# A two-layer max-aggregating graph network and an expert block: two tiles' late maxima and convolutions moved beside the last block steps of each layer

## The chip, the cores and the metric

The kernel runs on one core of one Trainium2 chip. A core has five engines that each work through their own instructions in order: TensorE (PE, matrix products), VectorE (DVE, elementwise work and maxima), ScalarE (ACT, copies and activations), GpSimd (POOL, here almost only the issuer of indirect gathers) and SyncE (SP, the issuer of plain transfers). PEld is TensorE's weight load. The metric is device time in microseconds (us); lower is better.

## The reference

1250 nodes with 512 features each, 20,000 random edges. The graph part is two layers of the same form, on layer-normalised rows:

```python
def _graph_conv_max(x, src, dst, W_rel, b, W_root):
    agg = jax.ops.segment_max(x[src], dst, num_segments=N)
    agg = jnp.where(jnp.isfinite(agg), agg, 0.0)
    return agg @ W_rel.T + b + x @ W_root.T
h = jax.nn.relu(_graph_conv_max(x, src, dst, W1_rel, b1, W1_root))
h = jax.nn.relu(_graph_conv_max(h, src, dst, W2_rel, b2, W2_root))
```

For every node this is the elementwise maximum over the rows of its neighbours, times one weight matrix, plus the node's own row times another. The result is added to `x`. Then comes an expert block: router logits, a softmax over the nodes, the top 512 nodes of each of eight experts, two matrix products per expert and a scatter back.

## The kernel before, in words

The nodes stand in NT = 10 tiles of TN = 125. Each layer has two phases, and the order of the instructions on each engine is the order of the program: a wrapper pins each call in program order (its line 34 is why every row of the profile says L34; rows are told apart by their buffers).

**The maximum of a tile** has three sources. *Block steps*: for destination tile t and source tile b, TensorE multiplies one-hot matrices (`ohs`) with the rows held as three bf16 parts (`xh`), six products into a PSUM bank of 125x1024; VectorE takes the maximum into `acc`. There are 10 x 10 steps, counted by `done`; step 10t+b+1 is the pair (t, b), its first step (b = 0) is copied by ScalarE, its last is followed by a fold (L640). Three PSUM banks (`pq` twice, `pair`) let TensorE run ahead. *Own rows*: what the blocks don't hold, seven gathered rows per node, from `table_d` by the index `nat_i`, as one group of four and one of three. *Late rows*: for nodes with still more neighbours; ten lists of falling length (34 down to 2), 30 groups of at most four rows; the maximum of each list goes to the DRAM tensor `late_d` (`ovf_d` in the profile), and every tile later gathers one row of it by `slot_i`.

**The first phase** (`first_phase`, L665) walks through a list of groups while the block steps run. Group n of `groups` is gathered by POOL into one of four `hb` buffers as soon as one is free, and merged by VectorE once `done` has reached `due`:

```python
due = lead + BEFORE + (n_steps - lead - BEFORE) * n // len(groups)
```

In layer one (lead 12) there are 34 groups: 30 late ones, n = 0 to 29, and the own groups of tiles 3 and 4, n = 30 to 33. Their due steps from n = 29 on are 87, 90, 92, 95, 97. In layer two (lead 10) there are 40: the same 30, then the own groups of tiles 0 to 4; due from n = 29 on are 76, 78, 80, 82, 84, 87, 89, 91, 93, 95, 97. The last late list, n = 29, has a single group of two rows; VectorE merges it and SyncE stores it to `late_d`. Before the last group is gathered, POOL asks for the late rows of tiles 0 to 3, four gathers into `wroot`, which has held W_root until then. Between the steps, pieces of the root product (`root_part`: the own row times W_root, stored to `root_d`) are handed out so that all are out at step 85.

**The second phase** (`second_phase`, L787) finishes the tiles. `own_rest(t)` gathers and merges the seven own rows of tiles 5 to 9, `backs` takes the late row into `acc`, and `ended(t)` transposes `acc` (`turn`), multiplies by W_rel (`conv`: eight products of 512 columns, four chunks by two passes, and the addition of the stored root part by an identity product) and hands over to a generator: in layer one `hidden` (ReLU, store to the other table, three bf16 parts), in layer two `residual` (ReLU plus `x`, moments, normalised row to `y_d`, transposed, logits). `on()` moves each waiting generator by one stage. The gathers of the second phase are 5 x 7 own rows and 6 late rows, 41 in all, on POOL's queue in program order, into the same four `hb` buffers. PSUM banks for transposes and for products are one each while the blocks run (`deep`), two each afterwards.

Of the kernel before, what the change touches and what calls it, by code (L numbers as in the profile page):

```python
# [23 lines left out]
class InOrder:  # L24


    def __init__(self, tc, engine):
        self.tc, self.engine = tc, engine
# [13 lines left out]
def fast_gnn(tc, ctx, sh, io, y_d):  # L42
# [283 lines left out]
    def turned(rows, dest):  # L326
        pt = bank("t")
        for c in range(KC):
            pe.transpose(pt[:, c, :TN], rows[:, c * P:(c + 1) * P], ident[:TN, :TN])
        act.copy(dest, pt[:, :, :TN])  # L330
# [202 lines left out]
    def grouped(rows):  # L533
        return [rows[j:j + G] for j in range(0, len(rows), G)]

    def own(layer, t):
        return [(table_d[layer], nat_i[:, t, k:k + 1]) for k in range(K0)]
# [102 lines left out]
    def block_steps(with_own):  # L640

        for t in range(NT):
            for b in range(NB):
                pq = bank("q")
                for r in range(R):
                    oh = ohs[:BR, t, (b * R + r) * TN:(b * R + r + 1) * TN]
                    for k in range(3):
                        pe.matmul(pq[:TN, r, :], oh, xh[:BR, b, k, :], start=(k == 0), stop=(k == 2))
                yield
                if b == 0:  # L650
                    acc2 = gk.tile([P, R, D], F32, name="acc2", bufs=2)
                    act.copy(acc2[:TN], pq[:TN])
                else:
                    dve.tensor_max(acc2[:TN], acc2[:TN], pq[:TN])
                if b == NB - 1:
                    if t in with_own:
                        folded(acc2, acc2[:TN, 0, :])
                        dve.tensor_max(acc[:TN, t, :], acc[:TN, t, :], acc2[:TN, 0, :])
                    else:
                        folded(acc2, acc[:TN, t, :])  # L660
                yield

    BEFORE = 4

    def first_phase(layer, lead, groups, lists, blocks, done):  # L665

        here = range(0 if layer else FRONT, NT)
        roots = in_turn([root_part(layer, t) for t in here])  # L670
        n_steps, given = NT * NB, 0
        def step():
            nonlocal done, given
            if layer == 0 and done % NB == 4 and done // NB + 2 < NT:
                onehots(done // NB + 2)
            if layer == 0 and done == NB + 2:
                own_early(2)
            next(blocks)
            done += 1
            while given < done * ROOT_PIECES * len(here) * 100 // (85 * n_steps):  # L680
                next(roots, None)
                given += 1
            next(blocks)

        deep[0] = True
        while done < lead:
            step()
        for n, (rows, i, fresh, whole) in enumerate(groups):
            due = lead + BEFORE + (n_steps - lead - BEFORE) * n // len(groups)
            for k in range(NT):  # L690
                if len(lists) < min(n + 3, NT) and k not in lists:
                    late_list(k)
                    lists.add(k)
            if 2 * n > len(groups) and weights[layer][2] is None:
                load_rel(layer)
            if n + 1 == len(groups):

                for k in range(G):
                    pool.indirect_dma_start(
                        out=wroot[:, k, :], out_offset=None, in_=late_d[:, :],  # L700
                        in_offset=bass.IndirectOffsetOnAxis(ap=slot_i[:, k:k + 1], axis=0))
            hb_g = gathers(rows)
            while done < due:
                step()
            if fresh:
                aw = wide()
            if len(rows) < 4 and fresh:
                dve.tensor_max(aw[:TN, 0, :], hb_g[0][:TN, 0, :], hb_g[0][:TN, 1, :])
                assert len(rows) == 2
                whole(aw, False)  # L710
                continue
            merged(hb_g, aw, fresh)
            if whole:
                whole(aw, True)
        while done < n_steps:
            step()
        deep[0] = False
        for _ in roots:
            pass
# [5 lines left out]
    def own_groups(layer, tiles):  # L725
        groups = []
        for t in tiles:
            parts_ = grouped(own(layer, t))
            for k, rows in enumerate(parts_):
                whole = (lambda aw, both, t=t: joined(aw, t)) if k + 1 == len(parts_) else None  # L730
                groups.append((rows, None, k == 0, whole))
        return groups

    def late_groups(layer):
        groups = []

        def kept(aw, both, i):
            ao = aw[:, 0, :]
            if both:
                ao = gk.tile([P, D], F32, name="line", bufs=LINES)  # L740
                folded(aw, ao[:TN])
            stored(late_d[i * TN:(i + 1) * TN, :], ao)

        for i in range(NT):
            parts_ = [[(layer, i, k) for k in range(CAPS[i])][j:j + G] for j in range(0, CAPS[i], G)]
            for k, rows in enumerate(parts_):
                whole = (lambda aw, both, i=i: kept(aw, both, i)) if k + 1 == len(parts_) else None
                groups.append((rows, i, k == 0, whole))
        return groups

    def conv(layer, t, agT):
        pm = bank("m")
        for c in range(KC):
            pe.matmul(pm[:TN], agT[:, c, :], weights[layer][2][:, c, :], start=(c == 0), stop=False)
        pe.matmul(pm[:TN], ident[:TN, :TN], ahead.pop(t)[:TN], start=False, stop=True)
        return pm
# [27 lines left out]
        head.logits(t, bank("t").rearrange("p c n -> p (c n)"))  # L784
        yield

    def second_phase(layer, finish, beside, between):  # L787

        going, turns = [], {}

        def on():
            for g in list(going):
                if next(g, True):
                    going.remove(g)

        def own_rest(t):
            aw = wide()
            for k, rows in enumerate(grouped(own(layer, t))):  # L800
                merged(gathers(rows), aw, k == 0)
            joined(aw, t)

        def backs(tiles, hb=None):
            if hb is None:
                hb, _ = gathers([(late_d, slot_i[:, t:t + 1]) for t in tiles])
            for k, t in enumerate(tiles):
                dve.tensor_max(acc[:TN, t, :], acc[:TN, t, :], hb[:TN, k, :])

        def turn(t):  # L810
            turns[t] = gk.tile([P, KC, TN], F32, name="turn", bufs=3)
            turned(acc[:TN, t, :], turns[t])

        def ended(*tiles):
            for t in tiles:
                if t not in turns:
                    turn(t)
                if t + 1 in ready:
                    turn(t + 1)
                g = finish(t, conv(layer, t, turns.pop(t)))  # L820
                next(g)
                on()
                if t + 1 == NT:
                    next(g)
                going.append(g)

        backs((0, 1, 2, 3), wroot)
        ready = {0, 1, 2, 3}
        ended(0)
        own_rest(5)  # L830
        ended(1)
        backs((4, 5))
        ready |= {4, 5}
        ended(2)
        own_rest(6)
        ended(3)
        own_rest(7)
        backs((6, 7))
        ready |= {6, 7}
        ended(4)  # L840
        own_rest(8)
        ended(5)
        own_rest(9)
        ended(6)
        backs((8, 9))
        ready |= {8, 9}
        beside()
        for t in (7, 8, 9):
            ended(t)
            between(t)  # L850
        while going:
            on()
            between(NT)

    first_phase(0, 12, late_groups(0) + own_groups(0, range(KEPT, EARLY)), set(),
                block_steps(set(range(KEPT))), 0)
    pbad = bank("m")
    pe.matmul(pbad[:1, :1], bads, ones_col, start=True, stop=True)
    dve.tensor_scalar(flag_i, pbad[:1, :1], 1.0, None, op0=ALU.min)
# [12 lines left out]
        for t in range(5):  # L872
            ready_block(t)

    second_phase(0, hidden, begun, ready_block)
    first_phase(1, 10, late_groups(1) + own_groups(1, range(EARLY)), set(range(NT)), blocks, ready_steps[0])

    words = ohs.rearrange("p t n -> p (t n)").bitcast(F32)[:, KC * N:]
    x_tiles = [words[:, k * D:(k + 1) * D] for k in range(6)]
# [11 lines left out]
        if t < NT:  # L891
            sp.dma_start(x_tiles[t % 6][:TN], x[t * TN:(t + 1) * TN, :])

    for t in range(3):
        fetch_x(t)
    head.load()

    def dense_begun():
        head.load_dense()
        head.constants()  # L900

    second_phase(1, residual, dense_begun, lambda t: head.begin(1) if t == NT else None)
    head.softmax()
    gctx.close()
    return acc, yT, flag_i, head
# [350 lines left out]
class Routing:  # L1256
# [180 lines left out]
    def beside(self, n=1):  # L1437
        for _ in range(n):
            next(self.steps, None)
# [404 lines left out]
```

## Time and profile before

| | |
|---|---|
| time, median of 3 runs | 889.24 us (889.02 to 891.01) |
| profiled execution's own time | 889.6 us |
| its span, first to last instruction | 887.9 us |
| mean granted TensorE clock | 0.942 |
| busy: PE / DVE / POOL / ACT | 695.0 / 629.2 / 533.5 / 159.5 us |
| gathers by the late lists / by own rows, on POOL | 214 at 1073 ns / 140 at 1057 ns |
| layer one: first phase ends (last fold), layer two's blocks alone begin | 303.2, about 390 us |
| layer two: first phase ends, last tile's convolution is under way | 600.6, about 675 us |

A row of the timeline has the start in us, the duration in us, the engine, the line, the operation, what it writes and reads, the shape, the count, and in brackets the idle time of the engine just before it with what ended that idle time. "issue" in the bracket means that nothing the profile shows was waited for. A group of rows with the same form that follow each other is merged. Gathers by POOL show the time of the issue; the data lands later. A product that writes `pq` or `pair` from `xh,ohs` is a block step; `acc<-acc,pq` is its maximum.

### The profile page before, as it was taken

How to read it: one execution, taken by the hardware profiler on the slowest of the kernel's cores; microseconds unless marked ns; L12 is line 12 of the kernel's file. 1: busy time of each engine (PE TensorE's matmuls, PEld its weight loads, DVE VectorE, ACT ScalarE, POOL GpSimd, SP SyncE). 2: the span in 40 equal slices, each digit the busy share in tenths (PEclk: the TensorE clock that was granted, in tenths of full speed). 3: DMA queues.
4: the chain of work that ended last, by engine and by line, in shares of the span. 5: the costliest groups of instructions: out<-in, count | busy, mean ns of one | idle time of the engine just before them, and what ended most of it. 6: DMA issues, size and time to landing. Idle time of an engine off the chain costs nothing. (4 is left out here: it accounts for less than half of the span.)

```text
span 887.9 us, 8334 instructions
## 1 busy us (share of the span) xinstructions
PE 695.0 (78%) x2534; PEld 374.1 (42%) x2534; DVE 629.2 (71%) x1156; ACT 159.5 (18%) x285; POOL 533.5 (60%) x547
## 2 busy tenths in 40 slices
PE   0599856777878688789788789758877888999992
PEld 0344433444445333345444445434434444444441
DVE  7799899999999945639899799987743554233211
ACT  2633000001000033130001011001223322112110
POOL 7552777777776876037777777777721401566542
PEclk9999989999999699899999999988989997999997
DMA  7676467978777588237977878877851404777753
GB/s 164 203 242 209 120 197 173 228 224 244 230 219 207 165 255 271 70 109 203 170 251 219 266 245 268 246 231 214 258 184 49 143 0 163 169 181 175 132 103 51
DMA packets 67784, 165.46 MB, mean 186 GB/s; under 512 B 12918, under 2 KB 17588, under 8 KB 67730
## 3 DMA queue, kind: packets, MB, share of 16 engines
q0 software_dynamic: 37472, 114.19, 49.1%
q1 hardware_dynamic: 29438, 49.55, 17.4%
q10 hardware_dynamic: 820, 1.10, 0.5%
q8 instruction: 22, 0.36, 0.2%
q14 instruction: 32, 0.26, 0.1%
HBM read 136.35 MB, written 28.40 MB: 186 GB/s over the span
## 5 line engine op out<-in xcount | busy, mean ns | idle before, releaser
L34 POOL DMA_INDIRECT hb<-table_d,late_i x214 | 229.6, 1073 | 105.4 <-issue 55.3
L34 PEld LDWEIGHTS <-ohs 126*125 126x125 bf16 (+1 forms) x1221 | 168.5, 139 | 226.1 <-issue 149.2
L34 PE MATMUL pq<-xh,ohs 126*125 126x512 bf16 x816 | 204.3, 393 | 57.8 <-DVE acc L34 47.4
L34 POOL DMA_INDIRECT hb<-table_d,nat_i x140 | 147.9, 1057 | 57.5 <-issue 36.9
L34 DVE TENSOR_TENSOR acc<-acc,pq 125x1024 f32<-125x1024 f32 x122 | 148.5, 1218 | 26.3 <-PE pq L34 19.5
L34 PE MATMUL pair<-xh,ohs 126*125 126x512 bf16 x384 | 96.1, 387 | 30.9 <-DVE acc L34 30.9
L34 POOL DMA_INDIRECT ysel<-y_d,idx x28 | 27.7, 988 | 77.4 <-issue 31.5
L34 DVE TENSOR_TENSOR acc<-acc,pair 125x1024 f32<-125x1024 f32 x58 | 70.5, 1216 | 3.8 <-PE pair L34 1.6
L34 DVE TENSOR_TENSOR wide<-wide,hb 125x1024 f32<-125x1024 f32 (+1 forms) x60 | 71.4, 1190 | 2.4 <-DMA hb<-table_d,late_i 0.6
L34 DVE TENSOR_TENSOR hb<-hb 125x1024 f32<-125x1024 f32 (+2 forms) x55 | 52.8, 961 | 24.9 <-DMA hb<-table_d,nat_i 18.0
L34 PE MATMUL pm<-wroot,turn 128*125 128x512 f32 x128 | 66.8, 607 | 0.4 <-ACT turn L34 0.4
L34 PE MATMUL pm<-yselT,w 128*128 128x512 f32 x112 | 52.4, 623 | 4.7 <-ACT yselT L34 4.7
L34 POOL DMA_INDIRECT out<-oo,idx x28 | 44.8, 1600 | 15.8 <-DVE oo L34 8.1
L34 PE MATMUL pm<-w,hT 128*128 128x512 f32 x112 | 52.7, 591 | 0.0
L34 DVE TENSOR_SCALAR oo<-pm,val 128x512 f32<-128x512 f32 x28 | 21.0, 751 | 44.0 <-PE pm L34 44.0
L34 DVE TENSOR_TENSOR wide<-hb 125x1024 f32<-125x1024 f32 (+1 forms) x40 | 47.8, 1196 | 4.9 <-DMA hb<-table_d,nat_i 3.4
L34 PE MATMUL pair<-wrel,turn 128*125 128x512 f32 x80 | 41.5, 667 | 9.9 <-ACT turn L34 7.7
L34 PE MATMUL pm<-wrel,turn 128*125 128x512 f32 x80 | 40.5, 653 | 3.3 <-DVE acc L34 3.3
L34 DVE COPY got<-pi 128x20 f32<-128x20 f32 x7 | 1.2, 178 | 52.4 <-PE pi L34 52.4
L34 PEld LDWEIGHTS pm<-yselT,w 128*128 128x128 f32 x112 | 21.6, 199 | 31.5 <-issue 25.0
L34 ACT COPY line<-pm 125x512 f32<-125x512 f32 x16 | 9.4, 586 | 137.4 <-PE pm L34 121.1
L34 PE MATMUL pair<-ident,acc 125*128 125x125 f32 x48 | 8.7, 312 | 32.2 <-ACT acc L34 18.5
(268 smaller groups left out, 877.5 us busy)
## 6 DMA issues: line engine op xcount, KB each, us to landing
w<-in_fw SPq DMA_DIRECT2D x14, 512.0 KB
ohs<-idx_d SPq DMA_DIRECT2D x10, 615.2 KB
root_d<-line SPq DMA_DIRECT2D x20, 250.0 KB
ahead<-root_d SPq DMA_DIRECT2D x20, 250.0 KB
table_d<-acc SPq DMA_DIRECT2D x20, 224.0 KB
ovf_d<-line SPq DMA_DIRECT2D x18, 224.0 KB
hb<-table_d,late_i POOLq DMA_INDIRECT x214, 5.1
ohs<-in_x SPq DMA_DIRECT2D x10, 250.0 KB
```

What stands on the lines that cost most here:

```text
L34: made = call(*args, **kwargs)
```

## The change

`second_phase` becomes a class `SecondPhase` that exists before the first phase starts, and `first_phase` takes `hooks`: functions called after given block steps.

- Layer one: after step 95 the late maxima of tiles 0 and 1, after step 96 `ended(0)`, after 98 the late maxima of tiles 2 and 3, after 99 `ended(1)`.
- Layer two: after step 75 the loads of three tiles of `x` and of the router weights, after 88 the late maxima of tiles 0 and 1, after 90 `ended(0)`, after 95 `ended(1)`, after 96 the late maxima of tiles 2 and 3. The root pieces are handed out by step 72 there.
- The four gathers of late rows into `wroot` stand before the gathers of group n = 31 (`n_late + 1`) in both layers, and any root pieces left are handed out ahead of them. Before, that was n = 33 in layer one and n = 39 in layer two.
- The rest of the second phase begins with two gathers, the late rows of tiles 4 and 5, into `wroot`, and goes on with tile 2.

```diff
-    def first_phase(layer, lead, groups, lists, blocks, done):
+    def first_phase(layer, lead, groups, n_late, lists, blocks, done, rooted, hooks):
...
-            while given < done * ROOT_PIECES * len(here) * 100 // (85 * n_steps):
+            while given < done * ROOT_PIECES * len(here) * 100 // (rooted * n_steps):
                 next(roots, None)
                 given += 1
             next(blocks)
+            if done in hooks:
+                hooks[done]()
...
-            if n + 1 == len(groups):
+            if n == n_late + 1:
+                for _ in roots:
+                    given += 1
 
                 for k in range(G):
                     pool.indirect_dma_start(
...
-        backs((0, 1, 2, 3), wroot)
-        ready = {0, 1, 2, 3}
-        ended(0)
-        own_rest(5)
-        ended(1)
-        backs((4, 5))
-        ready |= {4, 5}
-        ended(2)
-        own_rest(6)
-        ended(3)
...
+        def rest(self, beside, between):
+            late = wroot[:, 0:2]
+            for k in range(2):
+                pool.indirect_dma_start(
+                    out=late[:, k, :], out_offset=None, in_=late_d[:, :],
+                    in_offset=bass.IndirectOffsetOnAxis(ap=slot_i[:, 4 + k:5 + k], axis=0))
+            self.ended(2)
+            self.own_rest(5)
+            self.backs((4, 5), late)
+            self.ended(3)
+            self.own_rest(6)
+            self.ended(4)
+            self.own_rest(7)
+            self.backs((6, 7))
+            self.ended(5)
+            self.own_rest(8)
+            self.ended(6)
+            self.own_rest(9)
+            self.backs((8, 9))
+            beside()
+            for t in (7, 8, 9):
+                self.ended(t)
+                between(t)
...
+    second = SecondPhase(0, hidden)
+    first_phase(0, 12, late_groups(0) + own_groups(0, range(KEPT, EARLY)), len(late_groups(0)), set(),
+                block_steps(set(range(KEPT))), 0, 85,
+                {95: lambda: second.backs((0, 1), wroot), 96: lambda: second.ended(0),
+                 98: lambda: second.backs((2, 3), wroot[:, 2:4]), 99: lambda: second.ended(1)})
...
+    first_phase(1, 10, late_groups(1) + own_groups(1, range(EARLY)), len(late_groups(1)), set(range(NT)),
+                blocks, ready_steps[0], 72,
+                {75: head_begun, 88: lambda: layer2.backs((0, 1), wroot), 90: lambda: layer2.ended(0),
+                 95: lambda: layer2.ended(1), 96: lambda: layer2.backs((2, 3), wroot[:, 2:4])})
```

The order of `ended`, `on`, `backs`, `turn` and `own_rest` inside is the same as before, except that `ended` takes one tile and `backs` notes the tiles that are ready.

## The prediction

> **What bounds the kernel now.** I read the windows by stage first, then POOL's timeline where the moved gathers stand, then VectorE's beside it, then TensorE's convolution, and the same for layer two. The windows show microseconds, then busy time and count per engine:
>
> ```profile
> 278.00:303.20 25.20, 15.97 (x65) 9.12 (x63) 24.12 (x26) 1.01 (x1) 17.60 (x17) 0.87 0.69 195
> 303.20:354.50 51.30, 43.85 (x114) 20.58 (x115) 29.50 (x40) 15.29 (x27) 38.69 (x34) 0.87 0.79 239
> ...
> 545.90:600.60 54.70, 37.63 (x150) 21.72 (x147) 49.94 (x51) 3.44 (x5) 42.52 (x41) 0.90 0.80 242
> 600.60:655.00 54.40, 42.61 (x144) 22.67 (x145) 40.14 (x73) 13.02 (x30) 38.84 (x52) 0.91 0.75 229
> ```
>
> The columns after the length are PE, PEld, DVE, ACT, POOL. At the end of a first phase VectorE is full (24.12 of 25.20 us). In a second phase no engine looks full, but POOL's 38.7 us leave out 0.30 us of issue at each of 34 gathers: it has no real gap. So **first phases go at VectorE's pace and second phases at POOL's**. Now POOL in layer one:
>
> ```profile
> 269.55 0.95 POOL L34 DMA_INDIRECT hb<-table_d,nat_i  x1 [0.30 <-issue]
> 270.80 0.95 POOL L34 DMA_INDIRECT hb<-table_d,nat_i  x1 [0.30 <-issue]
> ...
> 278.86 0.95 POOL L34 DMA_INDIRECT hb<-table_d,nat_i  x1 [0.30 <-DMA ovf_d<-line]
> 282.83 1.36 POOL L34 DMA_INDIRECT wroot<-ovf_d,slot_i  x1 [3.03 <-DMA ovf_d<-wide]
> ...
> 287.49 1.15 POOL L34 DMA_INDIRECT wroot<-ovf_d,slot_i  x1 [0.30 <-issue]
> 288.94 0.95 POOL L34 DMA_INDIRECT hb<-table_d,nat_i  x1 [0.30 <-DVE acc L34]
> ...
> 291.45 0.94 POOL L34 DMA_INDIRECT hb<-table_d,nat_i  x1 [0.30 <-DMA wroot<-ovf_d,slot_i]
> ```
>
> 265.80 to 269.55 are the four rows of group 30, 270.80 to 273.30 the three of 31, 275.07 to 278.86 the four of 32. Then the late rows wait 3.03 us until the store of the last late list (`ovf_d<-wide`) has landed at 282.8. The reader is to see that POOL runs ahead of VectorE, and what is late when it gets there:
>
> ```profile
> 277.05 0.69 DVE L34 TENSOR_TENSOR wide<-hb 125x512 f32<-125x512 f32 x1
> ...
> 284.42 0.69 DVE L34 TENSOR_TENSOR hb<-hb 125x512 f32<-125x512 f32 x1
> ```
>
> 277.05 is the merge of group 29, at its due step 87; its store is issued at 277.76. 284.42 is the merge of group 31. Layer two, with the same marks:
>
> ```profile
> 540.32 0.94 POOL L34 DMA_INDIRECT hb<-table_d,nat_i  x1 [0.30 <-issue]
> 545.24 0.69 DVE L34 TENSOR_TENSOR wide<-hb 125x512 f32<-125x512 f32 x1
> 545.96 0.74 SPq L34 DMA_DIRECT2D ovf_d<-wide  x2
> ...
> 552.70 0.68 DVE L34 TENSOR_TENSOR hb<-hb 125x512 f32<-125x512 f32 x1
> ```
>
> POOL stands at group 31 (540.32) 5.6 us before the store it will now have to wait for is even issued.
>
> **The moved gathers, layer one.** All times below are on the clock of the profiled execution. Nothing before step 87 changes, so the store still lands at 282.8. In the new order POOL reaches the late rows after group 30, at 270.5, and stands for **12.3 us**, where it used to issue seven rows and wait 3.03. Behind it in its queue are groups 31, 32, 33 and the whole second phase. From 282.83 it issues the four late rows (6.1 us, as now: 282.83 to 288.94), then group 31 at 288.94, 290.19, 291.45. From last issue to merge, rows that VectorE waited for took 6.2 us (348.31 to 354.54) and 6.3 us (586.49 to 592.80); late rows on a quieter queue landed in 3.8 us. After a stall the queue is emptier, so I take 5.5: group 31 can be merged at 297, not 284.42. **VectorE stands for 12.6 us**, with steps 93 to 100 behind it, and TensorE behind those, for it has only three banks.
>
> **The hooks, layer one.** From 297: merge 31 takes 3.3 us, steps 93 to 95 3.9, late maxima of tiles 0 and 1 1.3, merge 32 1.2, step 96 1.3: 308. `ended(0)` stands on TensorE between the products of steps 96 and 97. What it costs there is in these rows:
>
> ```profile
> 303.88 1.09 PE L34 MATMUL pair<-ident,acc 125*128 125x125 f32 x4 [3.84 <-DVE acc L34]
> 304.77 1.04 PE L34 MATMUL pt<-ident,acc 125*128 125x125 f32 x4
> 305.69 5.88 PE L34 MATMUL pm<-wrel,turn 128*125 128x512 f32 x8
> 311.41 1.02 PE L34 MATMUL pm<-ahead,ident 125*125 125x512 f32 x2
> ...
> 319.06 3.60 PE L34 MATMUL pm<-wrel,turn 128*125 128x512 f32 x8
> ```
>
> From the first transpose to the end of the identity product is 8.5 us, with the eight products at 5.88 us after idling and at 3.60 warm. In the first phase the two turns share one bank, so the second waits for ScalarE's copy: 0.9 us more. The maxima end at 305.5; 305.6 + 8.5 + 0.9 + 1.5 for step 97's products gives 316.5, against 308: VectorE waits 8.5 us. Step 97, merge 33 (3.4), step 98, maxima of tiles 2 and 3, step 99 and one subtraction bring 325.7. `ended(1)` transposes tile 2 after those maxima (323.8), multiplies warm (0.6 + 3.6 + 1.0 + 1.5): step 100 comes at 330.5, a wait of 4.8. With step 100 and its fold the first phase ends at 332.4, where it ended at 303.2. Two tiles are through by then, but that was TensorE's work, and the second phase goes by POOL.
>
> The DMAs the hooks issue (two table stores and one `ahead` load per tile) have no late store behind them on SP: nothing. ScalarE is busy 1.01 of 25.2 us there: nothing, as long as its queue isn't full.
>
> **The second phase, layer one.** If only POOL's queue counted: ten rows of groups 31 to 33 from 288.94 end at 301.5; tiles 4 and 5's late rows wait for `wroot`, free at 305.5; then 16 rows at about 1.33 us: the first row of tile 7's own group at 327, now 317.47: **+9.5**. But that row needs an `hb` buffer, the one of tile 5's first group, which VectorE frees after the phase's end: 332.4, two subtractions 1.4, one maximum 1.2, so 335: **+17.9**. From there the 25 rows left follow as now, and so does the rest of the layer. Both ends stay in the range; as the four buffers are what ties POOL to VectorE, I take a value near the upper one: **+16**.
>
> **Layer two.** POOL stands from 540.0. The store issued at 545.96 lands at 551.0 (5.07 us as in layer one); three `x` tiles of 250 KB now go out on SP just before it, at 271 GB/s an estimated 0 to 2.8 us more; I take 1. Late rows 6.1 us, group 31 issued 558.1 to 560.6, merged at 566.1 for 552.70: VectorE stands **13.4 us**. From that merge to the end of the phase it worked 44.9 us (552.70 to 600.6, less waits of 0.39 and 2.60). Added: late maxima 2.5, tile 0's ReLU, sum and moments 1.75. The products of steps 91 and 92 come behind `ended(0)`: late maxima end at 585.8, two turns and a warm product (0.6 + 0.9 + 0.6 + 3.6 + 1.0 and two steps 2.8) make 596.3 where VectorE is there at 593.3: 3. `ended(1)` needs the single product bank, which tile 0's sum frees, and only then multiplies: 6.2 us against 2.3 of work, 4. The phase ends at 622, not 600.6. After 2.1 us of both residuals and 1.2 of a maximum the buffer for tile 7 is free at 625.6, now 608.73: **+16.9**. By POOL's queue alone: 28 rows at the present pace (540.32 to 577.70, 37.4 us), 3 and 16 more from 558.1: 620.4, **+11.7**. I take **+16** again.
>
> The faster hand-out of root pieces (4.1 us of TensorE per tile, over 72 steps instead of 85) adds 0.09 us per step, under VectorE's 2.3 us per step against some 1.9 of TensorE: nothing, at worst 1 us.
>
> **The sum.** 887.9 + 16 + 16 = 919.9 of span; the time lies 1.7 us above the span in the profiled execution and its 889.6 us within the runs shown. Against the median: 889.2 + 32 = **921**.
>
> **Two rules weighed.** The Trainium skill, "DMA: Bandwidth & Descriptors", "Anatomy of one DMA", gives a gather-path transfer 2.0 us plus the bytes at 436 GB/s: an estimated 2.6 us for the 250 KB of one gather. The rows above took 6.2 and 6.3 to the merge. By the rule group 31 would be there 2.9 us sooner in each layer and the time 915; the trace decides, since other transfers fill 0.8 of the DMA engines there. "TensorE: Matmul & The Clock Gate", "Part 1: The HAM clock gate", says an idle window of about 3.4 us halves the clock until about as long a busy time has passed. This speaks against the change: each stall of 12 us makes one more cold start. By the rule it costs at most 1.7 us; the row says 5.88 - 3.60 = 2.3, which I used for layer one. If layer two's is cold too: 923.
>
> **Rivals.**
> - *POOL's queue alone counts* (VectorE's waits lie under POOL's): +9.5 and +11.7, **910**. For it: POOL's brackets show "issue" nearly throughout. Against: four buffers.
> - *Everything in series*: cold products everywhere, VectorE's stalls fully passed on, the `x` loads in front of the store (2.8), rows landing in 6.3: +17.9 + 2 and +16.9 + 5, **931**.
> - *Faster*: the late store has landed when POOL comes to group 31. Then POOL loses nothing, the present waits of 3.03 (layer one) and 2.60 (VectorE for group 39) go, and 15 us of convolution leave a phase that POOL sets anyway: **884**. It decides if POOL arrives 12.3 us later, or the store lands that much sooner. POOL's 2.07 us wait for a buffer at 265.80 says that it is ahead, not behind.
> - *No change*: VectorE's slack swallows both stalls. It has 1.1 us in 25.2: **889**.
>
> **How the numbers follow.** The forecast has 0.50 (its own range 914 to 927), POOL alone 0.25 (904 to 914), series 0.18 (927 to 938), faster 0.05, no change 0.02. A range of 905 to 933 leaves out about 0.07 below and 0.08 above. A measurement of this kernel can tell 0.3% from no change, 2.7 us; faster 0.05, within 0.02, slower 0.93.
>
> **What would show it.** On POOL `wroot<-ovf_d` with about 12 us of idle before it, released by `ovf_d<-wide`, in both layers; `hb<-hb 125x512` of group 31 on VectorE waiting 11 to 14 us for `table_d,nat_i`; the last fold of layer one near 332; VectorE waiting for `pq` behind `wrel,turn` for 5 to 8 us in layer one; a wait of POOL for a buffer ahead of tile 7. The prediction is wrong if the store comes sooner than I have it, or if the second phase, with two tiles gone, no longer goes by POOL.

## The result, and the profile after

The changed kernel takes **919.83 us** (median of 4 runs, 918.59 to 922.75), the kernel before 889.13 us (888.34 to 891.01): a ratio of **1.0345, 95% interval 1.0317 to 1.0373**. The forecast was 921. The profiled execution has a span of 916.9 us against 887.9, 29.0 us more, with a mean granted TensorE clock of 0.923 against 0.942.

The windows view of the changed kernel comes first, with the columns as before (length, then PE, PEld, DVE, ACT, POOL, granted clock, DMA share, GB/s). The first row ends with layer one's first phase, the second with layer two's; the third is layer two's second phase.

```profile
278.00:324.30 46.30, 29.96 (x107) 15.96 (x106) 27.31 (x31) 6.26 (x10) 30.36 (x30) 0.85 0.68 196
...
554.80:633.00 78.20, 45.51 (x162) 24.72 (x161) 54.03 (x58) 3.38 (x5) 52.89 (x51) 0.82 0.69 201
633.00:685.00 52.00, 35.18 (x116) 18.95 (x115) 36.31 (x67) 11.46 (x27) 29.14 (x45) 0.80 0.70 216
```

VectorE, which filled 24.12 of 25.20 us at the end of layer one's first phase, is now busy for 27.31 of 46.30. The stretch holds two convolutions more and is 21 us longer, and most of that is standing. The timeline of the changed kernel in layer one, POOL's rows first and VectorE's behind them:

```profile
270.97 0.95 POOL L34 DMA_INDIRECT hb<-table_d,nat_i  x1 [0.30 <-issue]
281.21 0.95 POOL L34 DMA_INDIRECT wroot<-ovf_d,slot_i  x1 [9.29 <-PE pq L34]
...
288.72 0.94 POOL L34 DMA_INDIRECT hb<-table_d,nat_i  x1 [0.30 <-DMA wroot<-ovf_d,slot_i]
...
327.02 1.16 POOL L34 DMA_INDIRECT hb<-table_d,nat_i  x1 [5.57 <-DVE wide L34]
```

```profile
277.34 0.69 DVE L34 TENSOR_TENSOR wide<-hb 125x512 f32<-125x512 f32 x1
...
292.39 0.69 DVE L34 TENSOR_TENSOR hb<-hb 125x512 f32<-125x512 f32 x1 [7.54 <-DMA hb<-table_d,nat_i]
...
308.12 1.22 DVE L34 TENSOR_TENSOR acc<-acc,pq 125x1024 f32<-125x1024 f32 x1 [5.08 <-PE pq L34]
...
322.40 1.22 DVE L34 TENSOR_TENSOR acc<-acc,pq 125x1024 f32<-125x1024 f32 x1 [5.69 <-PE pq L34]
323.66 0.69 DVE L34 TENSOR_TENSOR acc<-acc 125x512 f32<-125x512 f32 x1
```

POOL comes to the late rows at 271.9, and the merge of group 29 that feeds their store begins only at 277.34. POOL stands for 9.29 us. Group 31, queued behind, is merged at 292.39, 15.05 us after that mark where it was 7.37. The two convolutions then cost VectorE 5.08 and 5.69 us, and POOL waits another 5.57 us for a buffer at tile 7's first own row. The profile names TensorE as what ended the first wait, but the last product that reads `wroot` had ended at 271.63, before POOL even came; experiments 3 and 10 show that the wait is for the store.

Layer two of the changed kernel, SP's, POOL's, VectorE's and TensorE's rows together in order of time:

```profile
552.60 1.22 SPq L34 DMA_DIRECT2D ohs<-in_x  x3
...
554.11 0.69 DVE L34 TENSOR_TENSOR wide<-hb 125x512 f32<-125x512 f32 x1
554.82 1.16 SPq L34 DMA_DIRECT2D ovf_d<-wide  x2
...
563.79 0.94 POOL L34 DMA_INDIRECT wroot<-ovf_d,slot_i  x1 [13.79 <-PE pq L34]
...
574.96 0.69 DVE L34 TENSOR_TENSOR hb<-hb 125x512 f32<-125x512 f32 x1 [13.40 <-DMA hb<-table_d,nat_i]
...
613.45 6.05 PE L34 MATMUL pm<-wrel,turn 128*125 128x512 f32 x8 [5.54 <-DVE acc L34]
...
621.69 1.22 DVE L34 TENSOR_TENSOR acc<-acc,pq 125x1024 f32<-125x1024 f32 x1 [5.91 <-PE pq L34]
...
636.62 1.15 POOL L34 DMA_INDIRECT hb<-table_d,nat_i  x1 [4.71 <-DVE wide L34]
...
653.07 0.28 DVE L34 TENSOR_REDUCE ohs<-ohs 128x1 f32<-128x125 f32 x1 [5.62 <-ACT ohs L34]
```

Here POOL stands for 13.79 us and VectorE for 13.40, three loads of `x` are issued 2.2 us ahead of the late store (with the load of the router weights between them and it), and the second convolution waits 5.54 us for its bank, is slow (6.05), and holds VectorE up for 5.91. The chain of waits in one table, from the waits view (engine and what it wrote, what it waited for, total us, times, longest); of the kernel before:

```profile
DVE ohs L34 <- ACT ohs L34: 26.0, 8, 6.6
DVE acc L34 <- PE pq L34: 19.5, 9, 6.2
DVE hb L34 <- DMA hb<-table_d,nat_i: 18.0, 6, 3.5
...
POOL hb L34 <- DVE wide L34: 4.3, 3, 2.1
```

and of the changed kernel:

```profile
DVE acc L34 <- PE pq L34: 39.3, 14, 7.3
DVE ohs L34 <- ACT ohs L34: 38.1, 9, 8.2
...
DVE hb L34 <- DMA hb<-table_d,nat_i: 28.7, 5, 13.4
POOL wroot L34 <- PE pq L34: 23.1, 2, 13.8
...
POOL hb L34 <- DVE wide L34: 19.6, 7, 5.6
```

VectorE's waits for block products and for gathered rows grew by 19.8 and 10.7 us. POOL stood 23.1 us at the late rows, where it was 3.0, and waited 15.3 us more for buffers.

Where the 29.0 us arise is read against one mark in each layer, the merge of group 29: the mark of layer two comes 8.9 us later (554.11 for 545.24), 0.3 of which was there at layer one's mark. The second mark of layer two is the row in which VectorE, behind the last late maxima, writes constants of the expert block, in the kernel before and in the changed one:

```profile
655.11 0.88 DVE L34 TENSOR_SCALAR ohs<-ohs 128x1 int32<-128x1 int32 x9
...
684.81 0.88 DVE L34 TENSOR_SCALAR ohs<-ohs 128x1 int32<-128x1 int32 x9
```

From mark to mark it is 20.8 us more (684.81 - 554.11 against 655.11 - 545.24), and the rest of the kernel, with the last three convolutions, gives 0.7 back: 0.3 + 8.6 + 20.8 - 0.7 = 29.0. So **layer one costs 8.6 us and layer two 20.8**.

### The profile page after: what moved, and what is told of

Read it like the earlier page. It is cut to its first block, busy times and chain, and to the rows that moved or that the text cites. A ratio compares the mean times of both kernels' runs of the same rounds, so it can differ in the third digit from the quotient of the medians.

```text
span 916.9 us, 8331 instructions
## 1 busy us (share of the span) xinstructions
PE 702.9 (77%) x2534; PEld 376.9 (41%) x2534; DVE 628.5 (69%) x1156; ACT 159.7 (17%) x285; POOL 526.5 (57%) x547
## 5 line engine op out<-in xcount | busy, mean ns | idle before, releaser
L34 PE MATMUL pair<-xh,ohs 126*125 126x512 bf16 x384 | 99.0, 396 | 39.4 <-DVE acc L34 39.4
L34 PE MATMUL pm<-wrel,turn 128*125 128x512 f32 x96 | 49.4, 662 | 6.6 <-DVE acc L34 6.6
L34 PE MATMUL pair<-wrel,turn 128*125 128x512 f32 x64 | 37.0, 731 | 4.1 <-ACT turn L34 2.7
L34 ACT COPY turn<-pt 128x500 f32<-128x500 f32 x31 | 17.9, 577 | 123.4 <-PE pt L34 123.4
L34 PE MATMUL pt<-ident,acc 125*128 125x125 f32 x124 | 21.5, 303 | 22.8 <-DVE acc L34 21.4
```

What stands on the lines that cost most here:

```text
L34: made = call(*args, **kwargs)
```

## The experiments

Two theories stand against each other. *The queue theory* (the forecast): POOL reaches the late rows before their store has landed, everything queued behind them is late, and VectorE with it. *The convolution theory* ("hook theory" in the expectations; a rival that the profile after suggested): the products of the hooks stand on TensorE's queue ahead of block products, and would cost VectorE the same without any wait on POOL. Later ones concern the `x` loads, the buffers and the product bank.

These kernels ran on two other chips, on which the kernel before takes 935.6 and 947.2 us. TensorE has pauses there for which the profile names no releaser ("issue"), and VectorE waits behind them ("issue", "remote"). So ratios to the kernel before on the same chip, and waits inside one trace, are compared, and not microseconds between chips; the only trace of the kernel before is from the first chip. Runs 1 to 8 are of one chip, 9 to 12 of the other.

**1 and 5. The gathers alone.** The kernel before, with only the late rows put ahead of group 31 in both layers, and no hooks:

```diff
-            if n + 1 == len(groups):
+            if n == 31:
+                for _ in roots:
+                    given += 1
...
-            while given < done * ROOT_PIECES * len(here) * 100 // (85 * n_steps):
+            while given < done * ROOT_PIECES * len(here) * 100 // ((72 if layer else 85) * n_steps):
```

> The kernel before, with only the four late-row gathers put ahead of group 31 in both layers (and the root pieces of layer two handed out by step 72); no hooks, second phase as before. Queue theory (POOL stands until the late store has landed, with seven and more rows behind it): about +9 us in layer one and +11 in layer two, 909 (905 to 913), with POOL idle some 9 us ahead of wroot in layer one and 11 in layer two. Hook theory (the convolutions between block steps cost the time): 889 to 893.

Measured: 947.7 us against 935.7, ratio 1.0204 (1.0048 to 1.0360). That is too wide to weigh a share. Run 5 is the same kernel once more:

> The kernel before with only the four late-row gathers ahead of group 31 in both layers (root pieces of layer two by step 72), no hooks; once more, since the kernel before ran unevenly beside its first run. Queue theory: POOL stands 9 us in each layer and seven or more rows wait behind it, +8 and +9: 906 against 889 (1.015 to 1.025 of the kernel before). Hook theory: 1.000 to 1.005.

Measured: 950.4 against 935.6, **1.0182 (1.0122 to 1.0242)**. POOL's late rows and VectorE's merge of group 31 in the second of these runs, layer one and layer two:

```profile
296.71 0.94 POOL L34 DMA_INDIRECT wroot<-ovf_d,slot_i  x1 [9.30 <-PE pq L34]
...
592.59 1.12 POOL L34 DMA_INDIRECT wroot<-ovf_d,slot_i  x1 [12.29 <-PE pq L34]
```

```profile
307.97 0.71 DVE L34 TENSOR_TENSOR hb<-hb 125x512 f32<-125x512 f32 x1 [7.63 <-DMA hb<-table_d,nat_i]
...
606.66 0.69 DVE L34 TENSOR_TENSOR hb<-hb 125x512 f32<-125x512 f32 x1 [10.58 <-DMA hb<-table_d,nat_i]
```

With no hook anywhere, POOL's stall and VectorE's wait are there, in layer one of the same size as in the changed kernel (9.29 and 7.54). The queue theory holds for this part. But the ratio is below the whole change's, whose intervals it doesn't touch on the first chip (1.0345) or in run 9 (1.0447): the moved gathers are not all of it, as far as ratios of different chips can say so.

**2. The late rows later.** The changed kernel, with the late rows back behind more groups, and layer one's hooks moved to the last steps so that the rows are there in time:

```diff
-            if n == n_late + 1:
+            if n == n_late + (5 if layer else 3):
...
-                {95: lambda: second.backs((0, 1), wroot), 96: lambda: second.ended(0),
-                 98: lambda: second.backs((2, 3), wroot[:, 2:4]), 99: lambda: second.ended(1)})
+                {97: lambda: second.backs((0, 1), wroot), 98: lambda: second.ended(0),
+                 99: lambda: second.backs((2, 3), wroot[:, 2:4]), 100: lambda: second.ended(1)})
```

> The changed kernel with the four late-row gathers ahead of group 33 in layer one (hooks there at steps 97 to 100 instead of 95 to 99) and of group 35 in layer two (hooks unchanged). Queue theory: POOL's long waits are gone (3 us in layer one as before, none in layer two), 889 to 898; what is left over 889 is the price of the hooks. Hook theory: 908 to 920.

Measured: 950.7 us, 1.0170 (0.9941 to 1.0399). By itself it decides nothing. Its trace does show that the edit was not enough: POOL's stall fell to 1.91 us in layer one, but in layer two 7.19 us are left. The store and the late rows that wait for it there:

```profile
585.28 5.35 SPq L34 DMA_DIRECT2D ovf_d<-wide  x2
...
601.27 0.94 POOL L34 DMA_INDIRECT wroot<-ovf_d,slot_i  x1 [7.19 <-PE pq L34]
```

POOL is released 19.9 us after the merge of group 29 began. The store was issued right behind the three `x` loads, and with POOL gathering for part of that time it took 16.0 us from there. Run 6 takes the loads away from in front of it.

**4. Layer two alone later.** The same, with `n_late + (5 if layer else 1)` and the hooks as in the changed kernel:

> The changed kernel with the four late-row gathers ahead of group 35 in layer two only; layer one as changed. Queue theory: layer one keeps its 9 us, layer two loses its wait of 13.8 us and keeps the waits for the convolutions: 899 to 907. Hook theory: 914 or more.

Measured: 957.5 us (945.4 to 966.6), too scattered for a verdict. POOL still stood 7.46 us in layer two, with the `x` loads in front of the store as in run 2, and 9.30 in layer one. Inconclusive.

**3. The `x` loads after the phase.** The changed kernel, with the three loads of `x` and the router weights behind the whole first phase. This leaves out the wait of tile 0's sum for its `x`, which is read before it is loaded:

```diff
-                {75: head_begun, 88: lambda: layer2.backs((0, 1), wroot), 90: lambda: layer2.ended(0),
+                {88: lambda: layer2.backs((0, 1), wroot), 90: lambda: layer2.ended(0),
...
+    head_begun()
```

> The changed kernel with the loads of x and of the router weights after layer two's first phase, as before. If they delay the late store (9.0 us from issue to POOL's release now, 5.1 in the trace before), POOL's wait falls by about 4 us and the time is 916 (914 to 918). If they don't: 920.

Measured: 968.5 us, 1.0437 (1.0285 to 1.0590). POOL's wait in layer two is 9.30 us, and it ends 3.95 us after the merge begins (590.58 to 594.53), where the changed kernel took 9.68. Only transfers on SP were moved, so the wait is for the store, whatever releaser the profile names. That the ratio is no lower than the changed kernel's on the first chip can't be weighed across chips, hence runs 9 and 10.

**9 and 10. The `x` loads, side by side.** Run 9 is the changed kernel itself, run 10 has the loads after step 80, behind the store:

```diff
-                {75: head_begun, 88: lambda: layer2.backs((0, 1), wroot), 90: lambda: layer2.ended(0),
+                {80: head_begun, 88: lambda: layer2.backs((0, 1), wroot), 90: lambda: layer2.ended(0),
```

> The changed kernel itself, beside the others of this call. If the parts add up (gathers alone 1.018, the rest 1.013), 1.030 to 1.036 of the kernel before, on whatever chip it runs.

> The changed kernel with the loads of x and of the router weights at step 80 of layer two instead of 75, behind the store of the last late list. Store theory: POOL's wait in layer two falls from 13.8 to about 9 us (release 4 us after the merge of the last late list instead of 9.7) and the time by 4 to 6 us against the changed kernel of this call. Rival (the wait is POOL's for something else): the same wait and time.

Measured: 986.1 us, 1.0447 (1.0357 to 1.0538), and 978.1, 1.0377 (1.0273 to 1.0482). SP's and POOL's rows, with the loads in front:

```profile
603.47 1.08 SPq L34 DMA_DIRECT2D ohs<-in_x  x3
...
605.70 0.76 SPq L34 DMA_DIRECT2D ovf_d<-wide  x2
...
614.00 0.94 POOL L34 DMA_INDIRECT wroot<-ovf_d,slot_i  x1 [20.47 <-PE pq L34]
```

and with the loads behind the store:

```profile
606.18 0.74 SPq L34 DMA_DIRECT2D ovf_d<-wide  x2
607.02 1.07 SPq L34 DMA_DIRECT2D ohs<-in_x  x3
...
609.43 1.13 POOL L34 DMA_INDIRECT wroot<-ovf_d,slot_i  x1 [9.31 <-PE pq L34]
```

From the store's issue to POOL's release it is 8.30 us in the one and 3.25 in the other: three loads of some 250 KB and that of the router weights in front of it cost the store **5.0 us**. In the trace this is plain; of the time the medians say 8 us, but the intervals overlap. Run 9 lies above its expectation of 1.030 to 1.036, which its interval only just touches: on this chip the parts of runs 5 and 6 come to less than the whole. POOL also stood longer than on the first chip, since it came to the late rows 11.5 us ahead of the merge of group 29 and not 4.1.

**6. Hardly a stall in either layer.** Runs 2 and 10 put together:

```diff
-            if n == n_late + 1:
+            if n == n_late + (5 if layer else 3):
...
-                {95: lambda: second.backs((0, 1), wroot), 96: lambda: second.ended(0),
-                 98: lambda: second.backs((2, 3), wroot[:, 2:4]), 99: lambda: second.ended(1)})
+                {97: lambda: second.backs((0, 1), wroot), 98: lambda: second.ended(0),
+                 99: lambda: second.backs((2, 3), wroot[:, 2:4]), 100: lambda: second.ended(1)})
...
-                {75: head_begun, 88: lambda: layer2.backs((0, 1), wroot), 90: lambda: layer2.ended(0),
+                {80: head_begun, 88: lambda: layer2.backs((0, 1), wroot), 90: lambda: layer2.ended(0),
```

> The changed kernel with the late rows ahead of group 33 in layer one (hooks at steps 97 to 100) and of group 35 in layer two, and the loads of x at step 80, behind the last late store. Queue theory: no long wait of POOL is left, 1.000 to 1.010 of the kernel before; what is over 1.000 is the price of the hooks. Hook theory: 1.02 or more.

Measured: 946.4 us, **1.0131 (1.0075 to 1.0188)**. POOL's stalls at the late rows are 2.20 and 0.30 us. What is left in layer two:

```profile
595.53 1.96 POOL L34 DMA_INDIRECT wroot<-ovf_d,slot_i  x1 [0.30 <-issue]
...
638.42 1.28 POOL L34 DMA_INDIRECT hb<-table_d,nat_i  x1 [6.63 <-DVE wide L34]
...
642.72 5.26 PE L34 MATMUL pm<-wrel,turn 128*125 128x512 f32 x8 [10.60 <-DVE acc L34]
...
650.17 1.22 DVE L34 TENSOR_TENSOR acc<-acc,pq 125x1024 f32<-125x1024 f32 x1 [5.13 <-PE pq L34]
```

The ratio lies between what the two theories said: without the stall the kernel is still slower than before. TensorE stands 10.60 us with the second convolution at the head of its queue, until VectorE has taken tile 0's sum out of the one product bank (the sum begins at 641.98); the block products are behind it, so VectorE then waits 5.13 us. POOL needs VectorE's merges for its buffers. Its wait of 6.63 us lies ahead of this convolution, behind two waits of VectorE (10.92 and 5.73 us) in which TensorE paused as it does on this chip; further waits of 3.10, 5.84 and 5.43 us follow. How much of the 1.3% is the hooks' own, and how much such pauses meeting them, is not shown.

**11. The bank emptied earlier.** Run 6 with one call more, which takes tile 0's sum three steps before the second convolution:

```diff
-                {80: head_begun, 88: lambda: layer2.backs((0, 1), wroot), 90: lambda: layer2.ended(0),
+                {80: head_begun, 88: lambda: layer2.backs((0, 1), wroot), 90: lambda: layer2.ended(0), 92: layer2.on,
```

> The run with late rows later and x behind, and one more hook: after step 92 of layer two the waiting generator of tile 0 moves on, so that its sum has freed the single product bank before tile 1's convolution at step 95. If that bank is what VectorE waits for behind the second convolution (5.9 us in the changed kernel): 3 to 5 us less, 1.004 to 1.010 of the kernel before. If the convolution's length is: within 2 us of 1.013.

Measured: 954.4 us against 947.2, **1.0081 (1.0048 to 1.0115)**, in its timeline:

```profile
601.55 1.96 POOL L34 DMA_INDIRECT wroot<-ovf_d,slot_i  x1 [0.30 <-issue]
...
641.04 3.60 PE L34 MATMUL pm<-wrel,turn 128*125 128x512 f32 x8
```

The second convolution starts with no wait, runs warm, and no wait of VectorE follows it: the single bank was what held it in run 6. The ratio is lower than run 6's, on another chip and with touching intervals, so the size of the gain is not settled. Against run 10 on the same chip (1.0377, intervals apart) it has hardly a stall of POOL (1.94 and 0.30 us), layer one's hooks one or two steps later and the bank freed, for 23.7 us less. Its ratio is the lowest of the versions with hooks, and still above 1.

**7 and 8. Are the buffers the tie?** The forecast held that the four `hb` buffers pass VectorE's lateness to POOL. Run 7 has five, with the room taken from two other pools; run 8 is its control, with the same room taken away and four buffers:

```diff
-    LINES = 6
+    LINES = 4
...
-    hp = gctx.enter_context(tc.tile_pool(name="hist", bufs=4))
+    hp = gctx.enter_context(tc.tile_pool(name="hist", bufs=5))
...
-                    acc2 = gk.tile([P, R, D], F32, name="acc2", bufs=2)
+                    acc2 = gk.tile([P, R, D], F32, name="acc2", bufs=1)
```

> The changed kernel with five gather buffers instead of four; room for it comes from one block-maximum tile instead of two and four line tiles instead of six. Buffer theory: POOL's waits for a buffer ahead of tile 7's own rows and after (5.6 us in layer one, 4.7 + 2.6 + 3.6 in layer two) go, 8 to 16 us less than the same kernel with four buffers. Rival (VectorE's stalls set the end anyway): within 3 us of it.

> The changed kernel with one block-maximum tile instead of two and four line tiles instead of six, and four gather buffers: the partner of the run with five. Smaller tiles cost 0 to 6 us over the changed kernel: 1.034 to 1.042 of the kernel before.

Measured: 987.0 us, 1.0584 (1.0513 to 1.0656), and 982.6, 1.0504 (1.0410 to 1.0598). With five buffers, the late rows and the longest wait for a buffer in layer two:

```profile
605.73 0.94 POOL L34 DMA_INDIRECT wroot<-ovf_d,slot_i  x1 [20.63 <-DMA ovf_d<-wide]
...
673.48 1.28 POOL L34 DMA_INDIRECT hb<-table_d,nat_i  x1 [10.14 <-DVE wide L34]
```

and with four:

```profile
611.41 0.94 POOL L34 DMA_INDIRECT wroot<-ovf_d,slot_i  x1 [15.58 <-PE pq L34]
...
674.91 1.27 POOL L34 DMA_INDIRECT hb<-table_d,nat_i  x1 [9.66 <-DVE wide L34]
```

A fifth buffer gains nothing where 8 to 16 us were expected. POOL only runs further ahead, comes to the late rows sooner and stands there 5 us longer; in layer two's second phase its waits for buffers add up to 29.4 us with five and 31.2 with four. So VectorE's lateness sets the pace, and a buffer more doesn't lift it. (With five buffers the profile does name the store as the releaser.) The control is a miss of its own, 1.0504 where 1.034 to 1.042 was expected; whether the smaller tiles or the chip make the difference is open.

**12. Layer two's hooks only.** Run 6, with layer one's hooks taken out and their calls put behind its first phase:

```diff
-                {97: lambda: second.backs((0, 1), wroot), 98: lambda: second.ended(0),
-                 99: lambda: second.backs((2, 3), wroot[:, 2:4]), 100: lambda: second.ended(1)})
+                {})
+    second.backs((0, 1, 2, 3), wroot)
+    second.ended(0)
+    second.ended(1)
```

> The run with late rows later and x behind, but in layer one the late maxima and the convolutions of tiles 0 and 1 come after the last block step, as before. If both layers' hooks have a price: 1.006 to 1.010 of the kernel before, half of the 1.013. If layer two's alone have it: 1.012 or more; if layer one's alone: 1.000 to 1.003.

Measured: 961.8 us, 1.0166 (1.0077 to 1.0254), no better than run 11. By the number alone layer two's hooks would have the whole price. POOL's late rows of tiles 4 and 5 in layer one show why it doesn't separate the layers:

```profile
324.19 1.15 POOL L34 DMA_INDIRECT wroot<-ovf_d,slot_i  x1 [11.63 <-DVE acc L34]
```

They go into `wroot`, which the late maxima of tiles 0 and 1 must have read; with those maxima behind the phase, POOL stands 11.63 us at the head of its second phase, where run 6 had 3.66. The same fault in another place, and the price of layer one's hooks alone stays open.

## Why the prediction was right, and where its terms were not

**What bounds the kernel.** That first phases go at VectorE's pace held. That second phases go at POOL's pace held only before the change: in layer two's second phase now POOL has 4.71, 2.64 and 3.61 us of waits for buffers, and VectorE waits behind the router's logits, in all 38.1 us where it was 26.0. Both things that the prediction named as signs of its being wrong so came to pass, although its number held: in layer two the second phase no longer goes by POOL, and in layer one the store came sooner.

**The moved gathers, layer one: the mechanism was right and its size too high.** Group 31 was to be merged 12.6 us later and came 7.7 later. The three terms that were off, each from the mark:

| | taken | measured |
|---|---|---|
| merge of group 29 to POOL's release | 5.8 | 3.9 |
| four late rows | 6.1 | 5.0 |
| last issue of group 31 to its merge | 5.5 | 3.7 |

I took all three from rows of the kernel before, where POOL kept gathering during the store. A POOL that stands sends nothing, and from the store's issue to the release the DMA engines were busy for a share of 0.40, where it was 0.81 before. In layer one the release came 3.9 us after the merge in all nine traces in which POOL stood from before the merge, and 5.8 to 6.2 us after it in the five in which it was still gathering then. So the stall shortens itself, by 4.8 us with all three terms. The 2.6 us that I had estimated for the gather from the Trainium skill ("DMA: Bandwidth & Descriptors", "Anatomy of one DMA") was too low and my 5.5 too high: 3.7 us stands nearer to the rule.

**The hooks, layer one.** VectorE was to wait 8.5 and 4.8 us at the two convolutions and waited 5.08 and 5.69. The first convolution ran warm, at a granted clock of 1.00, and the second partly cold, at 0.75:

```profile
302.32 3.60 PE L34 MATMUL pm<-wrel,turn 128*125 128x512 f32 x8
...
315.39 4.82 PE L34 MATMUL pm<-wrel,turn 128*125 128x512 f32 x8
```

I had it the other way round: block steps run between the stall and the first convolution, and before the second TensorE idles 3.86 us. The phase ends 20.9 us later (last fold at 323.66 for 302.48, less the 0.3 of the mark), for the 29.2 forecast. At tile 7's first own row I took +16 between ends of +9.5 and +17.9 (its 335 is in fact 17.5 after 317.47); it was **+9.3**. Its value is that of POOL's queue alone, but not its reason: POOL waited 5.57 us for VectorE's buffer there, and VectorE was 8 us less late than I had it. Layer one cost 8.6 us for 16.

**Layer two: the sum was nearly right, by two errors of opposite sign, and then it went on.** Group 31's merge was to come 13.4 us later and did. POOL was released 9.7 us after the merge where I had 6.8: the `x` loads cost some 5 us (runs 9 and 10), and I took 1 from a range of 0 to 2.8 worked out from bandwidth. Rows and landing were 2.9 us quicker, as in layer one. For the second convolution I took 4 us of VectorE's wait and warm products; it was 5.91, with the eight products at 6.05 and a granted clock of 0.61 over them, so the case "if layer two's is cold too" is what came. The cold clock cost 6.05 - 3.60 = 2.45 us; the Trainium skill's clock rule ("TensorE: Matmul & The Clock Gate", "Part 1: The HAM clock gate") gives an estimated 1.7 at most. For tile 7's row I took +16 from a worked +16.9; it was +19.0, 2.1 above, where the second convolution's wait alone was 1.9 above what I took. The layer's second mark came at +20.8, for POOL and VectorE have waits in the second phase that I had none of.

**The sum.** 16 + 16 stood against 8.6 + 20.8, with 0.3 at the first mark and -0.7 behind: 921 against 919.83. The total is right because layer one's cost was sized 7 us too high and layer two's 5 too low. The direction and the path were foreseen; that the sum came within 1.2 us is luck.

**The rivals.** *POOL's queue alone* (910) falls: POOL waits for VectorE in both layers. *Everything in series* (931) comes near for layer two's total alone, +21.9 for +20.8, though with rows that land in 6.3 us where they took 3.7. *Faster* rested on one condition, that POOL doesn't stall at the late rows, and was to give 884, or 0.994 of before. Runs 6 and 11 meet the condition in layer two and nearly in layer one, and give 1.0131 and 1.0081. So this rival fails, on those chips, for a reason that I hadn't given: the step in it that a convolution moved out of a phase set by POOL is free. The convolutions wait for VectorE at the head of TensorE's queue, with the block products of VectorE's own phase behind them; on the first chip this is the 5.08, 5.69 and 5.91 us of VectorE's waits.

**The shares.** The gathers alone cost 1.0182, the hooks without the stall 1.0131 or, with the bank freed, 1.0081. Added, with the `x` loads' 5 us on top, they come near the 1.0345 of the first chip, but run 9, the changed kernel on the chip of runs 10 to 12, took 1.0447. So the sum isn't closed to better than about one per cent. Open stay the price of layer one's hooks alone, what is left of run 11's 0.8%, and the nature of TensorE's pauses on the other chips. No version tried beats the kernel before.

## What to carry to other kernels

A gather that must wait for a store belongs as many entries behind it in the issuer's queue as the issuer runs ahead of the engine that makes the data: here one group behind the last late list left 9.3 to 13.8 us of standing on the first chip, three groups 3.03, and five groups 0.30 (run 6), or 7.19 with loads in front of the store (run 2). Before a load is hung on a step, look at which store stands behind it on the same queue and who waits for that store. Work moved beside a busier stage is not free if it shares a bank, or waits at the head of a queue in which that stage's work stands; no run here shows it free, for with the bank emptied in time (run 11) 0.8% stayed.

## What the hardware showed that I had not expected

- A standing POOL makes its own stall shorter: it was released 3.9 us after the merge and not 5.8, and the time from the last row's issue to the merge that waited for it was 3.7 us and not 6.2.
- Three loads of about 250 KB, issued 2.2 us ahead of a store on SP, kept it back for 5.0 us (8.30 against 3.25 from issue to release), nearly twice the 2.8 us that I had estimated from their bytes; why is open. With POOL gathering for part of the time (run 2), the store behind them took 16.0.
- TensorE's pauses on the other chips, in the waits view of the changed kernel on the chip of runs 9 to 12:

```profile
PE pq L34 <- issue: 29.9, 14, 7.1
PE pair L34 <- issue: 22.5, 10, 13.6
```

On the first chip the waits view has no such rows, before or after. On the chip of runs 9 to 12 the kernel before takes 6.5% longer, with the same program.
